# One layer slot reordered: both halves of P·V side by side, P's transposes into the third PSUM tile, the norm's Newton steps further down the vector queue

## The chip, the core and the metric

The kernel runs on one core of a Trainium2 chip. The time is what the device takes for one execution, in microseconds (us); the median of several executions is compared. The engines are named as the profile names them: PE is TensorE (PEld its weight loads), DVE is VectorE, ACT is ScalarE, POOL is GpSimd and SP is SyncE, which only issues DMAs here. Each engine runs its own queue in the order of the program and waits on semaphores where it needs another engine's result.

## The reference, cut to what matters

A causal attention block over 4 sequences of 512 tokens (width 128, 16 heads of 64) is followed by six layers. Each layer is local attention in windows of 32 tokens and a gated feed-forward network (FFN); both see their input with half of the features shifted by one token.

```python
def attn_layer(x, Wqkv, qs, ksc, Wo):          # x: 4 x 512 x 128
    q, k, v = split(x @ Wqkv)                  # 16 heads of 64
    q = l2norm(q) * qs
    k = l2norm(k) * ksc
    q = q * cos * scale + rotate_half(q) * sin * scale
    k = k * cos / scale + rotate_half(k) * sin / scale
    # every window of 32 tokens sees itself and the window before it
    sim = einsum('bhwie,bhwje->bhwij', q, look(k)) * 8
    out = einsum('bhwij,bhwje->bhwie', softmax(masked(sim)), look(v))
    return out @ Wo

def ffn_layer(x, g, bln, W1, b1, W2, b2):
    xn = (x - mean) / sqrt(var + 1e-05) * g + bln
    a, gate = split(xn @ W1 + b1)
    return a * gelu(gate) @ W2 + b2

for i in range(6):
    x = attn_layer(shift_tokens(x), ...) + x
    x = ffn_layer(shift_tokens(x), ...) + x
```

All of it is float32.

## The kernel before, in words

The first block (about the first 590 us) is not touched by the change. After it the work is cut into 96 **units**: layer, sequence b, and T, one of the four tiles of 128 tokens in a sequence. The function `slot` is called once for each unit, and the order of its calls is written out by hand: it is the order in which each engine's queue gets its instructions. Slot n works on several units at once, each at another stage:

- `new`, unit n+2: its three projections. `do_project(new, j)` with j = 0, 1, 2 for q, k, v is two products with 512 columns each (L477, of which the profile counts four). `square` (ACT, L488) and `sum_squares` (DVE, L493) give the squared norms. `rotate` is two DVE multiplications that read the projection in PSUM (L498 writes `rot`, L502 writes `t`). `add_rotated` (POOL, L513) adds them. `inverse_norms` takes 1/sqrt of the 32 sums: three short DVE instructions (L517, L80, L81), then twelve Newton steps on POOL (L83 to L86). `over_norm` (POOL, L521) scales. `v_windows` copies v out on ACT (L567), and SP issues 15 or 16 DMAs that spread it over the windows (`vw`).
- `nxt`, unit n+1: `transpose_q` and `transpose_k`, eight 128x128 transposes each (PE, L585) with two ACT copies (L588), and `carry_k` (POOL, L604), which hands the last 32 keys to the next unit.
- `u`, unit n: `scores` (the band mask L612 and the products L623, then DVE's maximum L633 and subtraction L635), `exponents` (ACT, L641), `transpose_p`, `times_v(u, 0)` and `times_v(u, 1)` (64 small products each, L655, then DVE's `rden` L664 and `on` L665), and `transpose_o`.
- `prev`, unit n-1: `project_out_2` (L680) and `residual` (L688).
- `now` and `last`, the FFN of the sequences before. With T = n % 4, `now` does `mean`, `var` and `scale` of its norm in the slots T = 1, 2, 3 (PE L94, L103, L111). `var` ends with `rsqrt`, that is L80, L81 and twelve Newton steps with four columns, all on DVE. `scale` is L115 and L117 on DVE. `chunk(0)` follows at T = 3; `last` does `chunk(1)`, `chunk(2)` and `out()` at T = 0, 1, 2 (L713 and L714, or L727), with DVE's L718 or L729 at the end.

`begin`, at the head of a slot, puts the shift of a coming sequence (L147 to L149) on POOL at T = 0, and once a layer also the rotary tables `lt` (L161).

PSUM decides what may overlap. Three tiles of two banks each rotate, `two_t(0)`, `two_t(1)`, `two_t(2)`; their roles move on by one from slot to slot. In a slot the first holds the scores, then v's projection, then the first half of P·V, then the FFN's chunk or `out()`. The second holds q's projection, then the second half of P·V. The third holds k's projection. Two single banks, `one_t()`, go round among the output projection, the norm, and all transposes. A tile is written again only when its readers are done: the second half of P·V waits for `rotate(new, 0)`, and the FFN's products wait for `on` of the first half.

Of the kernel before, what the change touches and what calls it, by code (L numbers as in the profile page):

```python
# [15 lines left out]
P = 128  # L16
# [4 lines left out]
NC = INNER // P  # L21
# [11 lines left out]
def body(ctx: ExitStack, tc: tile.TileContext, a, out: bass.AP):  # L33
# [5 lines left out]
    nc = tc.nc  # L39
# [3 lines left out]
    NT = S // P  # L43
# [31 lines left out]
    def rsqrt(v, n, eng):  # L75

        y = small.tile([P, n], F32, tag=f"y{n}", name="y")
        t = small.tile([P, n], F32, tag=f"yt{n}", name="yt")
        ti = t.bitcast(I32)
        nc.vector.tensor_scalar(ti, v.bitcast(I32), 1, None, ALU.logical_shift_right)  # L80
        nc.vector.tensor_scalar(y.bitcast(I32), ti, -1.0, 1597463007.0, ALU.mult, ALU.add)  # L81
        for k in range(3):
            eng.tensor_tensor(t, y, y, ALU.mult)  # L83
            eng.tensor_tensor(t, t, v, ALU.mult)
            eng.tensor_scalar(t, t, -0.5, 1.5, ALU.mult, ALU.add)
            eng.tensor_tensor(y if k < 2 else v, y, t, ALU.mult)  # L86

    def layernorm_steps(state, bank, inT, outT, g=None, b=None, eng=nc.vector):

        def mean():
            m = bank()
            mm(m, lhsT=avg, rhs=inT(), start=True, stop=True)  # L94
            xc = state["xc"] = tmpt()
            nc.vector.tensor_tensor(xc, inT(), m, ALU.subtract)
            sq = state["sq"] = tmpt()
            nc.scalar.activation(sq, xc, AF.Square)

        def var():  # L100
            v = bank()
            for t in range(NT):
                mm(v[:, t : t + 1], lhsT=state["sq"][:, t * P : (t + 1) * P], rhs=avg[:, 0:1], start=True, stop=True)  # L103
            rs = state["rs"] = small.tile([P, NT], F32, tag="rs", name="rs")
            nc.vector.tensor_scalar(rs, v[:, 0:NT], EPS, None, ALU.add)
            rsqrt(rs, NT, eng)

        def scale():
            bc = bank()
            for t in range(NT):  # L110
                nc.tensor.transpose(  # L111
                    bc[:, t * P : (t + 1) * P], state["rs"][:, t : t + 1].to_broadcast([P, P]), ident
                )
            h = state["h"] = outT()
            nc.vector.tensor_tensor(h, state["xc"], bc, ALU.mult)  # L115
            if g is not None:
                nc.vector.tensor_scalar(h, h, g, b, ALU.mult, ALU.add)  # L117

        return mean, var, scale

    xT = [None] * B

# [46 lines left out]
    with tc.manual_schedule():  # L169
# [70 lines left out]
        class Rows:  # L240
# [5 lines left out]
            def scores(self):  # L246
                b, c, t = self.b, self.c, self.t
                sc = self.sc = ps1.tile([P, 2, S], F32, tag="sc", name="ps_sc", bufs=2)
                for k0 in range(0, S, S // 2):
                    for h in range(2):  # L250
                        rows = slice(h * HD, (h + 1) * HD)
                        mm(
                            sc[:, h, k0 : k0 + S // 2],
                            lhsT=qs[b, c][rows, t * P : (t + 1) * P],
                            rhs=ks[b, c][rows, k0 : k0 + S // 2],
                            start=(k0 == 0),
                            stop=False,
                            skip_group_check=True,
                        )
# [23 lines left out]
            def exponents(self):  # L283
                self.pr = s1.tile([P, 2, S], F32, tag="pr1", name="pr1", bufs=3)
                self.den = small.tile([P, 2, 2], F32, tag="den", name="den")
                seen = (self.t + 1) * P
                for part_, cols in enumerate((slice(0, seen), slice(seen, S))):
                    for h in range(2):
                        if cols.start < S:
                            nc.scalar.activation(  # L290
                                self.pr[:, h, cols],
                                self.sc[:, h, cols],
                                AF.Exp,
                                bias=self.nm[:, part_, h : h + 1],
                                accum_out=self.den[:, part_, h : h + 1],
                            )
# [193 lines left out]
    def sum_squares(u, j):  # L490
        if j == 0:
            u.ss = small.tile([P, 2 * HEADS], F32, tag="ss", name="ss")
        nc.vector.tensor_reduce(u.ss[:, j * HEADS : (j + 1) * HEADS], heads(u.sq), AX.X, ALU.add)  # L493

    def rotate(u, j):
        t0 = u.r[j] = s2a.tile([P, INNER], F32, tag="rot", name="rot", bufs=6)
        lt, pf, half = u.lt, u.p[j], HD // 2
        nc.vector.tensor_tensor(  # L498
            heads(t0), heads(pf), lt[:, u.T, 2 * j].unsqueeze(1).to_broadcast([P, HEADS, HD]), ALU.mult
        )  # L500
        t1 = u.t1 = s2a.tile([P, INNER], F32, tag="t1", name="t1", bufs=3)
        nc.vector.tensor_tensor(  # L502
            t1.rearrange("p (h t d) -> p h t d", t=2, d=half),
            pf.rearrange("p (h t d) -> p h t d", t=2, d=half)[:, :, ::-1, :],
            lt[:, u.T, 2 * j + 1]
            .rearrange("p (t d) -> p t d", t=2)
            .unsqueeze(1)
            .to_broadcast([P, HEADS, 2, half]),
            ALU.mult,
        )  # L510
# [70 lines left out]
    def transposed(src, g, dst, col0):  # L581

        tp = one_t()
        for c in range(4):
            nc.tensor.transpose(  # L585
                tp[:, c * P : (c + 1) * P], src[:, (4 * g + c) * P : (4 * g + c + 1) * P], ident
            )
        nc.scalar.copy(dst[:, 4 * g : 4 * g + 4, col0 : col0 + P], tp.rearrange("p (c t) -> p c t", c=4))  # L588
# [53 lines left out]

    def transpose_p(u):
        u.pT = s2.tile([P, NC, P], F32, tag="pT", name="pT", bufs=2)
        for g in range(2):
            transposed(u.prf, g, u.pT, 0)

    def times_v(u, g):
        if g == 0:
# [43 lines left out]
    class Ffn:  # L693
        def __init__(self, i, b):
            self.i, self.b, self.us, self.st = i, b, [], {}
            self.mean, self.var, self.scale = layernorm_steps(
                self.st,
                one_t,
                lambda: self.xs,
                lambda: s2.tile([P, S], F32, tag="hT", name="hT", bufs=2),  # L700
                vecs[:, i, 0:1],
                vecs[:, i, 1:2],
            )

        def shift(self):
# [97 lines left out]
    def slot(n, now, last):  # L803

        u, prev, nxt, new = unit(n), unit(n - 1), unit(n + 1), unit(n + 2)
        T = n % NT
        part[0] = n % 3
        begin(unit(n + 4))  # L810
        if u:
            scores(u)
        if new:
            do_project(new, 0)
            square(new, 0)
        if n == -1:
            y = one_t()
            project_out1(B - 1, y)
        if u:
            exponents(u)  # L820
        if prev:
            project_out_2(prev)
            if prev.b + 1 == B and prev.T + 1 == NT and prev.i + 1 < L:
                wo_w[0] = load_wo(prev.i + 1)
        if new:
            sum_squares(new, 0)
        if prev:
            residual(prev)
        if now and T > 0:
            (now.mean, now.var, now.scale)[T - 1]()  # L830
        if now and T == 0:
            now.shift()
        if new:
            rotate(new, 0)
        if n == -1:
            residual1(B - 1, y)
        if new:
            do_project(new, 2)
            v_windows(new, follower(new))
        if u:  # L840
            transpose_p(u)
        if new:
            add_rotated(new, 0)
            do_project(new, 1)
            square(new, 1)
        if u:
            times_v(u, 0)
        if new:
            sum_squares(new, 1)
        if nxt:  # L850
            transpose_q(nxt)
        if u:
            times_v(u, 1)
        if new:
            inverse_norms(new)
            over_norm(new, 0)
        if nxt:
            transpose_k(nxt)
        if new:
            rotate(new, 1)  # L860
            add_rotated(new, 1)
            over_norm(new, 1)
        if n == -1:
            third_step()
        if nxt:
            carry_k(nxt, follower(nxt))
        if now and T == 3:
            now.chunk(0)
        if last:
            (lambda: last.chunk(1), lambda: last.chunk(2), last.out)[T]()  # L870
        if u:
            transpose_o(u)
# [106 lines left out]
```

## Time and profile before

| | |
|---|---|
| Time before, median of 3 runs | 2278.62 us (2278.29 to 2281.74) |
| Profiled execution | 2281.5 us, its span 2279.7 us |
| PE, DVE, ACT, POOL busy | 2178.0, 1729.1, 1347.6, 1451.3 us |
| Mean granted TensorE clock | 0.993 |
| From one band product to the next (a slot), median at T = 0, 1, 2, 3 | 16.6, 17.1, 18.7, 16.6 us |

The span runs from the first to the last instruction of the profiled execution. In a line of the timeline the first number is the start, the second the time that the instructions take, then come the engine, the source line, the operation, what is written from what, the count, and in brackets the idle time of the engine before it and who ended it. Line numbers are those of the kernel before.

### The profile page before, as it was taken

Reading aid. Unit: us, or ns where it says so; the run is one execution under the profiler, and the core shown is the slowest. Engines: PE = TensorE matmul, PEld = TensorE weight load, DVE = VectorE, ACT = ScalarE, POOL = GpSimd, SP = SyncE. Lnnn points to the kernel's source line nnn. Section 1 sums busy time; section 2 is a strip of 40 time slices with the busy share of each in tenths; the row PEclk is TensorE's granted clock in tenths of the full one; section 3 lists DMA queues with packets and bytes.
Section 4 is the critical chain, followed back from the end, with each engine's and each line's share of the span. In section 5 each row is a group of like instructions: output and inputs, shape, how many; then the busy total and the mean of one; then the engine's idle time right before and its main releaser. Section 6 shows DMA issues by size and latency. Waiting matters only on the chain.

```text
span 2279.7 us, 82205 instructions
## 1 busy us (share of the span) xinstructions
PE 2178.0 (96%) x35088; PEld 1435.6 (63%) x35088; DVE 1729.1 (76%) x2800; ACT 1347.6 (59%) x2550; POOL 1451.3 (64%) x1981
## 2 busy tenths in 40 slices
PE   6999999999999999999999999999999999999997
PEld 3555555555566666666666666666666666666664
DVE  3776667767778787878887788878888878888774
ACT  3665655655455656666566666666656666666562
POOL 1544545455877677767677777677776667766760
PEclk8999999999999999999999999999999999999998
DMA  3000000000322233232322323222332223222220
GB/s 115 1 1 1 1 1 1 1 1 1 75 70 64 63 88 75 58 75 68 87 67 64 77 70 91 64 62 69 85 85 56 72 63 88 73 67 70 65 56 15
DMA packets 91029, 125.74 MB, mean 55 GB/s; under 512 B 25390, under 2 KB 39468, under 8 KB 90668
## 3 DMA queue, kind: packets, MB, share of 16 engines
q1 hardware_dynamic: 90236, 118.92, 21.1%
q8 instruction: 279, 4.57, 0.9%
q10 hardware_dynamic: 432, 1.57, 0.2%
q14 instruction: 82, 0.67, 0.1%
HBM read 20.31 MB, written 1.05 MB: 9 GB/s over the span
## 4 chain that ended last, share of the span: by engine, by line
PE 63%; DVE 9%; issue 2%; ACT 1%; POOL 0%; POOLq 0%; ACTq 0%
PE ps_proj L477 19%; PE ps_one L585 14%; PE ps_one L680 7%; PE ps_att L655 6%; PE ps_att L623 6%; PE ps_proj L713 3%; PE ps_proj L714 3%; PE ps_proj L727 2%; DVE yt L80 2%; DVE t L502 1%; DVE rot L498 1%; PE ps_att L612 1%; PE ps_one L94 1%; PE ps_one L103 1%; DVE yt L83 1%
## 5 line engine op out<-in xcount | busy, mean ns | idle before, releaser
L513 POOL TENSOR_TENSOR rot<-rot,t 128x1024 f32<-128x1024 f32 x192 | 453.8, 2364 | 197.5 <-DVE t L502 185.9
L477 PE MATMUL ps_proj<-wqkv,xs 128*128 128x512 f32 x1152 | 553.3, 603 | 4.3 <-DVE t L502 2.8
L304 POOL TENSOR_TENSOR pr<-pr,den 128x1024 f32<-128x1024 f32 x128 | 240.9, 1893 | 266.9 <-DVE den L301 258.6
L488 ACT ACTIVATE sq<-ps_proj 128x1024 f32<-128x1024 f32 x192 | 196.8, 1025 | 356.7 <-PE ps_proj L477 324.5
L521 POOL TENSOR_TENSOR rot<-rot,ss 128x1024 f32<-128x1024 f32 x192 | 365.2, 1902 | 14.9
L477 PEld LDWEIGHTS ps_proj<-wqkv,xs 128*128 128x128 f32 x1152 | 198.1, 190 | 166.1 <-issue 146.5
L493 DVE TENSOR_REDUCE ss<-sq 128x16 f32<-128x1024 f32 x192 | 233.1, 1214 | 46.9 <-ACT sq L488 46.3
L498 DVE TENSOR_TENSOR rot<-ps_proj,lt 128x1024 f32<-128x1024 f32 x192 | 233.6, 1217 | 0.0
L502 DVE TENSOR_TENSOR t<-ps_proj,lt 128x1024 f32<-128x1024 f32 x192 | 233.2, 1215 | 0.4 <-POOL rot L513 0.4
L290 ACT ACTIVATE pr<-ps_sc,nm 128x128 f32<-128x128 f32 (+3 forms) x448 | 220.1, 507 | 20.0 <-DVE nm L279 16.7
L279 DVE TENSOR_REDUCE nm<-ps_sc 128x2 f32<-128x1024 f32 x128 | 156.0, 1219 | 91.0 <-PE ps_sc L267 91.0
L585 PE MATMUL ps_one<-ident,rot 128*128 128x128 f32 x1536 | 211.3, 280 | 5.9 <-issue 4.4
L680 PEld LDWEIGHTS ps_one<-aT,wo 128*128 128x128 f32 x1536 | 186.3, 192 | 45.3 <-issue 44.5
L83 POOL TENSOR_TENSOR yt<-y 128x32 f32<-128x32 f32 (+1 forms) x309 | 72.9, 236 | 210.5 <-DVE y L81 194.3
L633 DVE TENSOR_REDUCE mx<-ps_att 128x16 f32<-128x1024 f32 x96 | 117.5, 1224 | 102.3 <-PE ps_att L623 102.2
L680 PE MATMUL ps_one<-aT,wo 128*128 128x128 f32 x1536 | 187.3, 275 | 0.4 <-ACT aT L588 0.4
L585 PEld LDWEIGHTS ps_one<-ident,rot 128*128 128x128 f32 x1536 | 165.3, 141 | 25.3 <-issue 7.1
L319 ACT COPY pT<-ps_pt 128x512 f32<-128x512 f32 x128 | 75.5, 590 | 176.2 <-PE ps_pt L315 176.2
L655 PEld LDWEIGHTS ps_att<-vw,pT 64*32 64x32 f32 x9216 | 103.5, 105 | 93.4 <-ACT pT L588 54.0
L567 ACT COPY vt<-ps_proj 128x512 f32<-128x512 f32 x192 | 103.2, 590 | 93.6 <-PE ps_proj L477 91.6
L315 PEld LDWEIGHTS ps_pt<-ident,pr 128*128 128x128 f32 x1024 | 117.6, 142 | 56.7 <-issue 47.6
L655 PE MATMUL ps_att<-vw,pT 64*32 64x65 f32 x9216 | 129.0, 225 | 24.2 <-DVE t L502 13.4
(134 smaller groups left out, 4062.3 us busy)
## 6 DMA issues: line engine op xcount, KB each, us to landing
vw<-vt SPq DMA_DIRECT2D x1152, 65.0 KB
vw_first<-vt SPq DMA_DIRECT2D x336, 65.0 KB
wqkv<-in_wqkv_dram SPq DMA_DIRECT2D x18, 512.0 KB
wo<-in_wo_dram SPq DMA_DIRECT2D x6, 512.0 KB
w<-in_w_dram SPq DMA_DIRECT2D x6, 341.0 KB
xr<-in_x_dram SPq DMA_DIRECT2D x4, 256.0 KB
out_dram<-tmp_t SPq DMA_DIRECT2D x4, 256.0 KB
w<-in_w_dram SPq DMA_DIRECT2D x12, 64.0 KB
```

What stands on the lines that cost most here:

```text
L290: nc.scalar.activation(self.pr[:, h, cols], self.sc[:, h, cols], AF.Exp, bias=self.nm[:, part_, h : h + 1], accum_out=self.den[:, part_, h ...
L304: nc.gpsimd.tensor_tensor(self.pr, self.pr, self.den[:, 0].unsqueeze(2).to_broadcast([P, 2, S]), ALU.mult)
L477: mm(p[:, c, :], lhsT=u.xs[:, u.T * P : (u.T + 1) * P], rhs=wpart[j][:, c * 512 : (c + 1) * 512], start=True, stop=True,)
L488: nc.scalar.activation(u.sq, u.p[j], AF.Square)
L493: nc.vector.tensor_reduce(u.ss[:, j * HEADS : (j + 1) * HEADS], heads(u.sq), AX.X, ALU.add)
L498: nc.vector.tensor_tensor(heads(t0), heads(pf), lt[:, u.T, 2 * j].unsqueeze(1).to_broadcast([P, HEADS, HD]), ALU.mult)
L502: nc.vector.tensor_tensor(t1.rearrange("p (h t d) -> p h t d", t=2, d=half), pf.rearrange("p (h t d) -> p h t d", t=2, d=half)[:, :, ::-1, :],
L513: nc.gpsimd.tensor_tensor(u.r[j], u.r[j], u.t1, ALU.add)
L521: nc.gpsimd.tensor_tensor(heads(u.r[j]), heads(u.r[j]), u.ss[:, j * HEADS : (j + 1) * HEADS].unsqueeze(2).to_broadcast([P, HEADS, HD]), AL ...
L585: nc.tensor.transpose(tp[:, c * P : (c + 1) * P], src[:, (4 * g + c) * P : (4 * g + c + 1) * P], ident)
L655: mm(o[j * W : (j + 1) * W, h, c * (HD + 1) : (c + 1) * (HD + 1)], lhsT=u.pT[h * HD : (h + 1) * HD, 4 * g + c, j * W : (j + 1) * W], rhs=u ...
L680: mm(y[:, 0:P], lhsT=wo_w[0][:, c, :], rhs=u.aT[:, c, :], start=(c == 0), stop=(c == NC - 1))
```

## The change

Three things are reordered in `slot`, and nothing is computed differently.

1. `times_v(u, 0)` and `times_v(u, 1)` stand together, after `transpose_q` and before k's projection; before, q's transposes stood between them. k's projection, `square(new, 1)`, `rotate(new, 1)`, `add_rotated(new, 1)`, `sum_squares(new, 1)`, `inverse_norms` and both `over_norm` come after them, the POOL work after `carry_k`.
2. `transpose_p` writes its eight transposes into `two_t(2)` instead of the two single banks, and both ACT copies follow the last transpose.
3. The norm's `rsqrt` is a fourth step, `roots`, called at T = 2 after `rotate(new, 0)`, `add_rotated(new, 0)` and `sum_squares(new, 0)`.

`exponents(u)` also moves ahead of q's projection, and `sum_squares(new, 0)` behind `rotate(new, 0)`.

```diff
@@ layernorm_steps
             rs = state["rs"] = small.tile([P, NT], F32, tag="rs", name="rs")
             nc.vector.tensor_scalar(rs, v[:, 0:NT], EPS, None, ALU.add)
-            rsqrt(rs, NT, eng)
+            if not apart:
+                roots()
+
+        def roots():
+            rsqrt(state["rs"], NT, eng)
...
@@ transpose_p
         u.pT = s2.tile([P, NC, P], F32, tag="pT", name="pT", bufs=2)
+        tp = two_t(2, "ps_att")
+        for c in range(NC):
+            nc.tensor.transpose(
+                tp[:, c // 4, c % 4 * P : (c % 4 + 1) * P], u.prf[:, c * P : (c + 1) * P], ident
+            )
         for g in range(2):
-            transposed(u.prf, g, u.pT, 0)
+            nc.scalar.copy(u.pT[:, 4 * g : 4 * g + 4], tp[:, g].rearrange("p (c t) -> p c t", c=4))
...
@@ slot
         if u:
             scores(u)
+            exponents(u)
         if new:
             do_project(new, 0)
             square(new, 0)
...
-        if u:
-            exponents(u)
         if prev:
             project_out_2(prev)
...
-        if new:
-            sum_squares(new, 0)
-        if prev:
             residual(prev)
...
         if new:
             rotate(new, 0)
+            add_rotated(new, 0)
+            sum_squares(new, 0)
...
+        if now and T == 2:
+            now.roots()
         if new:
             do_project(new, 2)
             v_windows(new, follower(new))
         if u:
             transpose_p(u)
-        if new:
-            add_rotated(new, 0)
-            do_project(new, 1)
-            square(new, 1)
-        if u:
-            times_v(u, 0)
-        if new:
-            sum_squares(new, 1)
         if nxt:
             transpose_q(nxt)
         if u:
+            times_v(u, 0)
             times_v(u, 1)
         if new:
-            inverse_norms(new)
-            over_norm(new, 0)
+            do_project(new, 1)
+            square(new, 1)
         if nxt:
             transpose_k(nxt)
-        if new:
-            rotate(new, 1)
-            add_rotated(new, 1)
-            over_norm(new, 1)
         if n == -1:
             third_step()
         if nxt:
             carry_k(nxt, follower(nxt))
+        if new:
+            rotate(new, 1)
+            add_rotated(new, 1)
+            sum_squares(new, 1)
+            inverse_norms(new)
+            over_norm(new, 0)
+            over_norm(new, 1)
```

More of the change, by code (lines that the diff above doesn't have):

```diff
@@ L86, in rsqrt, with layernorm_steps @@
             eng.tensor_tensor(y if k < 2 else v, y, t, ALU.mult)
-    def layernorm_steps(state, bank, inT, outT, g=None, b=None, eng=nc.vector):
+    def layernorm_steps(state, bank, inT, outT, g=None, b=None, eng=nc.vector, apart=False):
         def mean():
@@ L117, in scale @@
                 nc.vector.tensor_scalar(h, h, g, b, ALU.mult, ALU.add)
-        return mean, var, scale
+        return (mean, var, scale, roots) if apart else (mean, var, scale)
     xT = [None] * B
@@ L695, in __init__ @@
             self.i, self.b, self.us, self.st = i, b, [], {}
-            self.mean, self.var, self.scale = layernorm_steps(
+            self.mean, self.var, self.scale, self.roots = layernorm_steps(
                 self.st,
@@ L702, in __init__ @@
                 vecs[:, i, 1:2],
+                apart=True,
             )
```

## The prediction

> **What bounds the kernel now.** I read four views, in this order. First the page: busy time and the chain that ended last.
>
> ```profile
> PE 2178.0 (96%) x35088; PEld 1435.6 (63%) x35088; DVE 1729.1 (76%) x2800; ACT 1347.6 (59%) x2550; POOL 1451.3 (64%) x1981
> ...
> PE 63%; DVE 9%; issue 2%; ACT 1%; POOL 0%; POOLq 0%; ACTq 0%
> ```
>
> TensorE (PE) carries the chain, so in the layers a slot (one unit of 128 tokens) lasts as long as its PE work plus PE's waits. I then read the timeline between successive band products (L612), which open every slot: median 16.6 us at T=0, 17.1 at T=1, 18.7 at T=2 and 16.6 at T=3. T=2 has two more products (L727), 0.86 us; about 0.8 us more is a wait. The timeline of one T=2 slot (start 1445.17) shows it:
>
> ```profile
> 1451.60 1.90 POOL L521 TENSOR_TENSOR rot<-rot,ss 128x1024 f32<-128x1024 f32 x1
> 1451.63 0.16 DVE L105 TENSOR_SCALAR rs<-ps_one 128x4 f32<-128x4 f32 x1
> 1451.83 1.70 DVE L80 TENSOR_SCALAR yt<-rs 128x4 int32<-128x4 int32 x1
> ...
> 1456.17 1.22 DVE L498 TENSOR_TENSOR rot<-ps_proj,lt 128x1024 f32<-128x1024 f32 x1
> 1456.73 1.09 PE L585 MATMUL ps_one<-ident,rot 128*128 128x128 f32 x8
> 1457.30 1.21 DVE L502 TENSOR_TENSOR t<-ps_proj,lt 128x1024 f32<-128x1024 f32 x1
> ...
> 1458.57 0.86 PE L655 MATMUL ps_att<-vw,pT 64*32 64x65 f32 x64 [0.74 <-DVE t L502]
> ```
>
> The norm's root stands on VectorE (DVE) ahead of `rotate(new, 0)`: L80 to the last L86 take 4.3 us (1451.83 to 1456.17). `rotate` therefore ends at 1458.51, and only then may the second half of P·V write the bank that q's projection held. Note L80: 1.70 us for four columns, where the 128x32 form has a median of 0.18. It ended when GpSimd's (POOL's) L521 ended (1453.50).
>
> The same thing is seen once a layer with other instructions, where POOL is late:
>
> ```profile
> 1633.87 2.35 POOL L513 TENSOR_TENSOR rot<-rot,t 128x1024 f32<-128x1024 f32 x1
> 1633.97 2.29 DVE L517 TENSOR_SCALAR ss<-ss 128x32 f32<-128x32 f32 x1
> 1636.29 0.18 DVE L80 TENSOR_SCALAR yt<-ss 128x32 int32<-128x32 int32 x1
> 1636.51 0.18 DVE L81 TENSOR_SCALAR y<-yt 128x32 int32<-128x32 int32 x1
> 1636.60 1.22 DVE L498 TENSOR_TENSOR rot<-ps_proj,lt 128x1024 f32<-128x1024 f32 x1
> ```
>
> A small tensor_scalar of DVE stands still until the POOL instruction that runs beside it is over. The rotations, which read PSUM, keep 1.21 to 1.22 us whatever POOL does.
>
> [...]eight transposes take 0.87 us from start to start beside whole-array work, 1.02 to 1.03 between the two halves of P·V, 0.93 after one.
>
> **The change, part by part.** Times within a slot count from its band products. Pitches from the PE timeline: scores 1.85, projection 1.82 after a tiled block and 1.72 otherwise, output projection 1.78, norm 0.86/0.81/0.44 (T=1/2/3), eight transposes 0.87, half of P·V 0.79, an FFN chunk 1.72, L727 2.58.
>
> *P·V in one block.* Before: P 0.87, projection of k 1.81, half 0.79, q 1.03, half 0.79, K 0.93, sum 6.22. After: P 0.87, q 0.96, halves 1.58, projection 1.82, K 0.87, sum 6.10. That is -0.12 in each of some 93 slots. P's transposes go to the third tile, whose chunk of the slot before is long read; ScalarE (ACT) copies them out by about 10.2, before k's projection needs the tile (11.5). q's transposes cover those copies except for some 0.1.
>
> *Exponentials ahead of q's projection in program order* (its square follows on ACT): at T=0 the table load (1.28) no longer stands between square and exponentials, and a PE wait of 0.2 before P's transposes goes (the V projection there has a pitch of 1.92). SP's 15 or 16 copies to `vw` follow the same ACT copies at the same point of the slot and are read two slots later: nothing.
>
> *`sum_squares(new, 0)` behind `rotate(new, 0)`*: 1.14 of DVE off rotate's path; outside T=2 nothing waited there.
>
> *The POOL chain.* Each instruction of the k side now comes after k's projection, which is itself later. At T=1: projection ends 13.3; rotate on DVE 13.5 to 15.85; ACT squares (1.02) before it copies K out, so `carry_k`, now ahead of `add_rotated(new, 1)` on POOL, runs 15.7 to 16.15; the add 16.2 to 18.55 (2.36). `inverse_norms` is now issued 0.7 us behind the start of that add: L517 is ready at 17.0 and stands still until 18.55, in every slot and not once a layer. L81 starts at 19.0, POOL's twelve Newton steps at 19.3 (12 x 0.32), over_norm at 23.1 and 25.0, end 26.85, which is 10.1 us into the T=2 slot. In the kernel before, over_norm(1) ended at 8.3 of that slot.
>
> *Roots later, T=2.* DVE: rotate(0) 6.65 to 8.95, its sum of squares to 10.05, then the roots. POOL's add_rotated(0) starts at 10.1 and ends at 12.45. L80 or, if that slips through, L81 stands still until then; twelve steps of 0.2 give 15.0. Queued behind the roots is rden/on of the first half (0.24 + 0.69): 15.9. The order of instructions confirms that `last.out`'s first product waits for DVE: it writes the tile that this half holds. PE is ready at 1.85+1.82+1.78+0.81+1.72+0.87+0.96+1.58+1.82+0.87 = 14.1. New wait: 1.8 us, in place of 0.8. T=2: -0.12 + 1.0 = +0.9.
>
> *T=3 after it.* rotate(1) now runs 16.8 to 19.1, the blocked L517 ends at 21.6, the residual L729 holds DVE to 22.8, while the scores are done at 19.5 + 1.85 = 21.4. The maximum starts 1.4 late; the subtraction ends about when V's projection wants the tile (+0.1). The norm's L117, also a tensor_scalar in SBUF, comes 4.0 to 4.1 us after L81, and over_norm(0) starts 0.26 + 3.86 = 4.1 us after it: a toss-up. If L117 is second it waits 1.9, rotate(0) ends at 11.1 and the second half of P·V, due at 10.3, waits 0.8; if first, nothing.
>
> *T=0*: the 0.2 gained goes again on V's projection waiting for the late subtraction and q's transposes for over_norm (0.1 each).
>
> *Once a layer* POOL's `lt` (2.37) stands before add_rotated(0) and now pushes the whole chain to q's transposes: +0.8, five times.
>
> Sum per four slots: T=0 -0.1, T=1 0, T=2 +0.9, T=3 +0.1 or +0.9; together +0.9 or +1.7. Over 23 sequences +21 or +39, with the layers' +4: +25 or +43. The toss-up taken in the middle: **+33 us**. The profiled execution has 2279.7 us of span and 1.8 around it, 2281.5; that gives 2314.5. It ran 2.9 above the median of 2278.6, so I predict **2311 us**.
>
> [...]
>
> **Rivals.**
> *The roots meet an idle POOL (faster).* [...]the roots end at 12.5 and `on` at 13.4, before PE wants it at 14.1. T=2 then gains 0.9, T=3 none or 0.1: with T=0 and T=1 about -1.2 per four slots, -28 us, 2251 us. For it: L80 on `ss` has a median of 0.18 where POOL is idle. Against: in all T=2 slots L80 took 0.94 to 1.84, and POOL has work queued at that point. It decides if `on` ends before 14.1, so if add_rotated(0) ends before 10.6 instead of 12.45.
>
> *The two waits are equal (no change).* If over_norm ends 1 us earlier than laid out, add_rotated(0) ends at 11.4 and the new wait is 0.8; savings and the rest of T=3 cancel: within 5 us, 2276.
>
> *POOL's chain sets every slot (much slower).* From k's projection to q's transposes the chain takes 0.2+2.35+2.4+0.75+3.9+1.9, and PE's 0.96+1.58+1.82 back to the end of that projection: 15.9, plus carry_k's delay 0.3, so 16.2 against PE's own 15.95 at T=0 and 16.8 at T=1. With 0.3 more on POOL, all slots but T=2 lengthen: +0.65 per slot, 2340 us. For it: equality at T=0. Against: T=1 and T=2 have slack.
>
> **How the numbers follow.** A measurement of this kernel can tell about 0.2%, 4.6 us, from no change. Port wait at the roots and at L517, 0.75: 2311, own range 2293 to 2332. Much slower 0.06. Equal waits 0.06, of which 0.04 within the bound, the rest either side of it. Idle POOL 0.13. The range, 2268 to 2338, takes in the equal waits and part of the way to 2251. Faster 0.14, same 0.04, slower 0.82.
>
> **What would show it.** At T=2: L80 or L81 on `rs` at 2 us and more behind L513; the wait of L655 for DVE `t` gone, and a wait of `last.out`'s products for DVE `on` of 1.5 to 2 us. L517 with a mean near 1.7 us instead of 0.21. No transposes of 1.03 us between halves of P·V. At T=3 L117 either near 2 us, with the second half waiting for `t`, or near 0.3. If L80 on `rs` stays under 1 us and `last.out` doesn't wait, the forecast is wrong and the faster rival holds.

## The result, and the profile after

The changed kernel takes 2427.21 us (median of 6 runs, 2420.58 to 2435.3) against 2280.53 us for the kernel before on the same chips (6 runs, 2278.29 to 2281.91). The ratio is 1.0646, with a 95% interval of 1.0624 to 1.0669: slower by 147 us. The forecast was 2311, with a range of 2268 to 2338. The direction was right; the loss is over four times as large as forecast (33), and outside the range.

In the changed file the source lines named here lie 5 to 11 further down: scores L628 (before L623), subtraction L640 (L635), P·V L665 (L655), `rden`/`on` L674/L675, square L493, `sum_squares` L498, `rotate` L503/L507, `add_rotated` L518, `inverse_norms` L522, `over_norm` L526, scale of the norm L122 (L117), projection L482, transposes of P L652 with their copies L656, other transposes L590 with copies L593, `out()` L738. L80 and L81 keep theirs.

The first view is the page of the changed kernel: busy time, and the chain that ended last.

```profile
PE 2249.6 (93%) x35088; PEld 1511.9 (62%) x35088; DVE 1834.2 (76%) x2800; ACT 1319.2 (54%) x2550; POOL 1456.8 (60%) x1981
...
PE 43%; DVE 22%; issue 6%; ACT 4%; POOL 2%; SPq 0%; DMA 0%; ACTq 0%; POOLq 0%
```

With the same instructions, PE counts 72 us more and DVE 105 us more, PE's share of the chain falls from 63% to 43%, DVE's rises from 9% to 22%, and "issue", where an engine waits for nothing that the profile shows, from 2% to 6%. (PE's ends are modelled, and the count of products is the same: a longer busy time here means the same products drawn out, not more work.) The loss stands in the layers: from the first band product to the last it is 145 us. Of this, 6.5 us lie in the first slot and 8.7 in two slots near the end; in the other slots a mean of 17.3 us has become 18.7. Where the slots lose, in mean us from start to start over 20 or 21 slots each (the first eight and the last six of the 96 left out):

| | T=0 | T=1 | T=2 | T=3 |
|---|---|---|---|---|
| slot, before | 16.60 | 17.24 | 18.57 | 17.03 |
| slot, after | 17.71 | 19.16 | 20.41 | 17.80 |
| both halves of P·V, before | 1.79 | 1.70 | 1.61 | 2.04 |
| both halves of P·V, after | 2.27 | 3.03 | 2.86 | 2.99 |

P·V has 4.0 of the 5.6 us per four slots. The waits of PE over the layers (PE and what it writes, line, releaser: us in all, times, longest; "issue" as the releaser means that the profile shows none) show one half of this. Of the kernel before:

```profile
PE ps_att L655 <- DVE t L502: 13.4, 18, 1.5
PE ps_att L655 <- issue: 10.1, 12, 1.6
...
PE ps_att L623 <- issue: 6.2, 14, 1.7
```

and of the kernel after:

```profile
PE ps_att L665 <- issue: 47.0, 27, 2.6
PE ps_att L628 <- issue: 20.5, 28, 2.0
PE ps_proj L738 <- DVE rden L674: 15.2, 14, 2.0
PE ps_proj L482 <- DVE pr L640: 14.1, 19, 1.4
```

The wait for `t` has gone, and the wait of `out()` (L738) for DVE has come, as laid out in the prediction. But the largest idle time of PE stands inside P·V and inside the scores, and no semaphore ends it. The timeline of T=1 and the start of T=2 (slots at 1433.16 and 1452.95) shows the rest:

```profile
1444.67 1.09 ACT L656 COPY pT<-ps_att 128x512 f32<-128x512 f32 x2
1445.33 2.31 PE L665 MATMUL ps_att<-vw,pT 64*32 64x65 f32 x128
...
1449.65 1.03 ACT L493 ACTIVATE sq<-ps_proj 128x1024 f32<-128x1024 f32 x1 [2.91 <-PE ps_proj L482]
1450.71 1.23 DVE L503 TENSOR_TENSOR rot<-ps_proj,lt 128x1024 f32<-128x1024 f32 x1 [1.91 <-ACT sq L493]
1453.15 2.36 POOL L518 TENSOR_TENSOR rot<-rot,t 128x1024 f32<-128x1024 f32 x1 [1.05 <-DVE t L507]
1454.22 1.32 DVE L522 TENSOR_SCALAR ss<-ss 128x32 f32<-128x32 f32 x1
```

This P·V has no gap, and yet it lasts 2.31 us, 2.24 from its start to the next block's; two halves alone took 2 x 0.79 from start to start. And DVE's rotation L503 starts 0.03 us after ACT's square L493 has ended: it stands still for a reader of the same PSUM tile. L522 then starts 1.07 us into POOL's L518 and ends 0.03 us after it. This is what the prediction calls the port wait; that a port is what holds these instructions is not shown. From 600 us on, 23 of the 25 L80 with four columns take over 0.5 us in the kernel before and end 0.02 to 0.03 us after a POOL instruction that ran beside them, and in the kernel after all 94 L522 end 0.04 us after L518. Divided into stretches of 0.4 us (busy PE and PEld with their instructions, clock, DMA share, GB/s), one P·V of the changed kernel goes like this:

```profile
1445.30:1445.70 0.40, 0.37 (x7) 0.37 (x8) 1.00 0.82 328
1445.70:1446.10 0.40, 0.40 (x10) 0.40 (x8) 1.00 0.93 369
1446.10:1446.50 0.40, 0.40 (x39) 0.40 (x37) 1.00 0.72 264
1446.50:1446.90 0.40, 0.40 (x61) 0.40 (x41) 1.00 0.80 249
```

Its first 17 products take 0.8 us, the pace after that is several times as high. The clock granted is full (1.00) all the while. The head of the block is slow.

### The profile page after: what moved, and what is told of

Same layout as the page of the kernel before. It is cut to its first block, busy times and chain, and to the rows that moved or that the text cites. A ratio compares the mean times of both kernels' runs of the same rounds, so it can differ in the third digit from the quotient of the medians.

```text
span 2425.6 us, 82264 instructions
## 1 busy us (share of the span) xinstructions
PE 2249.6 (93%) x35088; PEld 1511.9 (62%) x35088; DVE 1834.2 (76%) x2800; ACT 1319.2 (54%) x2550; POOL 1456.8 (60%) x1981
## 4 chain that ended last, share of the span: by engine, by line
PE 43%; DVE 22%; issue 6%; ACT 4%; POOL 2%; SPq 0%; DMA 0%; ACTq 0%; POOLq 0%
PE ps_proj L482 15%; PE ps_att L665 7%; PE ps_one L590 5%; PE ps_one L690 3%; DVE rot L503 3%; DVE t L507 3%; DVE ss L498 3%; PE ps_att L628 3%; ACT sq L493 3%; DVE ss L522 3%; PE ps_proj L738 2%; DVE pr L640 2%; PE ps_att L652 2%; DVE mx L638 2%; DVE yt L80 1%
## 5 line engine op out<-in xcount | busy, mean ns | idle before, releaser
L518 POOL TENSOR_TENSOR rot<-rot,t 128x1024 f32<-128x1024 f32 x192 | 453.5, 2362 | 260.2 <-DVE t L507 244.9
L482 PE MATMUL ps_proj<-wqkv,xs 128*128 128x512 f32 x1152 | 579.4, 626 | 21.5 <-DVE pr L640 17.4
L503 DVE TENSOR_TENSOR rot<-ps_proj,lt 128x1024 f32<-128x1024 f32 x192 | 234.6, 1222 | 236.9 <-ACT sq L493 236.6
L493 ACT ACTIVATE sq<-ps_proj 128x1024 f32<-128x1024 f32 x192 | 194.9, 1015 | 346.3 <-PE ps_proj L482 345.6
L526 POOL TENSOR_TENSOR rot<-rot,ss 128x1024 f32<-128x1024 f32 x192 | 365.2, 1923 | 7.4
L482 PEld LDWEIGHTS ps_proj<-wqkv,xs 128*128 128x128 f32 x1152 | 199.5, 192 | 204.1 <-issue 160.9
L646 ACT ACTIVATE pr<-pr 128x1024 f32<-128x1024 f32 x96 | 101.5, 1057 | 356.1 <-DVE pr L640 356.1
L507 DVE TENSOR_TENSOR t<-ps_proj,lt 128x1024 f32<-128x1024 f32 x192 | 233.2, 1214 | 6.9 <-POOL rot L518 6.9
L498 DVE TENSOR_REDUCE ss<-sq 128x16 f32<-128x1024 f32 x192 | 232.0, 1208 | 0.0
L590 PEld LDWEIGHTS ps_one<-ident,rot 128*128 128x128 f32 x1536 | 179.0, 144 | 65.3 <-issue 54.4
L665 PE MATMUL ps_att<-vw,pT 64*32 64x65 f32 x9216 | 172.2, 226 | 45.3 <-issue 42.9
L590 PE MATMUL ps_one<-ident,rot 128*128 128x128 f32 x1536 | 207.1, 279 | 2.9 <-POOL rot L526 1.7
L665 PEld LDWEIGHTS ps_att<-vw,pT 64*32 64x32 f32 x9216 | 150.7, 106 | 65.2 <-issue 46.2
L675 DVE TENSOR_TENSOR on<-ps_att,rden 128x512 f32<-128x512 f32 x192 | 132.8, 692 | 6.6
L320 PE MATMUL ps_pt<-ident,pr 128*128 128x128 f32 x1024 | 134.6, 274 | 3.0 <-POOL pr L309 2.9
```

The lines of the kernel that those rows point to most:

```text
L320: nc.tensor.transpose(pt[:, k * P : (k + 1) * P], self.pr[:, h, k * P : (k + 1) * P], ident)
L482: mm(p[:, c, :], lhsT=u.xs[:, u.T * P : (u.T + 1) * P], rhs=wpart[j][:, c * 512 : (c + 1) * 512], start=True, stop=True,)
L493: nc.scalar.activation(u.sq, u.p[j], AF.Square)
L503: nc.vector.tensor_tensor(heads(t0), heads(pf), lt[:, u.T, 2 * j].unsqueeze(1).to_broadcast([P, HEADS, HD]), ALU.mult)
L507: nc.vector.tensor_tensor(t1.rearrange("p (h t d) -> p h t d", t=2, d=half), pf.rearrange("p (h t d) -> p h t d", t=2, d=half)[:, :, ::-1, :],
L518: nc.gpsimd.tensor_tensor(u.r[j], u.r[j], u.t1, ALU.add)
```

## The experiments

Three theories for the slow block. **D**: its first eight products, two for each of the four windows, wait on the semaphores of the DMAs that filled `vw`. These have long landed (those issued in the slot before 1357.67 had moved their data by 1362, and the P·V that reads them starts at 1386.46), but most waits are an instruction of their own on PE's queue. The line view of the kernel after has them (durations in ns, shortest, median and longest; first and last start):

```profile
L665 PEldq EVENT_SEMAPHORE  x691: 51/51/51, 726.2 to 2267.3; - x173
```

**S**: 128 small products in a row (and their 128 weight loads) outrun the supply of instructions. **T** (the theory, not the tile number): the DMA traffic of that stretch slows the products. The expectations name a fourth, **V**: the chain of DVE and POOL has become longer. If it were that alone, none of the edits to P·V would help.

**a_split: the two halves apart again.** In the kernel after, k's projection between them.

```diff
             times_v(u, 0)
-            times_v(u, 1)
         if new:
             do_project(new, 1)
+        if u:
+            times_v(u, 1)
+        if new:
             square(new, 1)
```

> The changed kernel with one edit: k's projection stands between the two halves of P.V, so no more than 64 small products follow one another. Measured for the changed kernel: 2427 us; 25 gaps in the 128-product block in which PE waits for nothing that the profile shows, 44 us together, and a block pitch of 2.2 us where it has no such gap. Theory S (a run of 128 products, 256 PE instructions with their weight loads, outruns the supply of instructions): the gaps fall to about what the kernel before had in its halves (7 us), and the time by 35 to 50 us, to 2375 to 2390. Theory D (the first eight products each wait for DMAs, and nothing covers that any longer): the first half still takes 1.3 to 1.4 us instead of 0.8, second half 0.8. Theory V (the vector and GpSimd chain is what became longer): within 10 us of 2427.

Measured: 2370.89 us, ratio to the kernel before 1.0396 [1.038, 1.0411], 56 us less than the kernel after and so more than V allows.

```profile
PE ps_att L665 <- issue: 4.8, 8, 2.0
```

The gaps in P·V fall from 47.0 to 4.8 us, as S has it. The first half still takes 1.31 (T=0) to 1.58 us (T=1), the second 0.79 by median: the slow head stays with the first half, as D has it. Two different things had been put together.

**b_join: the halves joined in the kernel before.** k's projection and q's transposes then stand ahead of the block, and nothing else is changed.

```diff
             square(new, 1)
-        if u:
-            times_v(u, 0)
         if new:
             sum_squares(new, 1)
...
         if u:
+            times_v(u, 0)
             times_v(u, 1)
```

> The kernel before with one edit: both halves of P.V stand together, after q's transposes; k's projection and q's transposes still lie between P's transposes and the block. Theory S: gaps of about 2 us in the block as in the changed kernel, some 25 of them, time 2310 to 2330. Theory D: the waits are dealt with while PE still works on the projection, the block pitch is 1.6, time 2265 to 2280 ([...]the wait at T=2 in the same place). Theory V: the same as D.

Measured: 2298.49 us, ratio 1.0074 [1.0055, 1.0093], between the ranges of S and D. By median the block takes 1.53 to 1.69 us at T=0, T=1 and T=3 (at T=2 it waits for `t` and takes 2.72): the head is not slow here, with the same DMA waits. The difference is in what stands ahead. In one slot of b_join, ACT's copies of P are done 1.56 us before the block:

```profile
1431.37 1.10 ACT L588 COPY pT<-ps_one 128x512 f32<-128x512 f32 x2
...
1434.03 1.64 PE L655 MATMUL ps_att<-vw_first,pT 64*32 64x65 f32 x128
```

In the kernel after, the block starts before the second of these copies is done (1445.33 against 1445.76, above). PE's queue stands at the wait for P until PE has run dry (0.32 us of idle time of PEld before the block, ended by the first copy), and the DMA waits come only then. In b_join the queue goes through them while PE still works on k's projection and q's transposes (1431.35 to 1434.03). The line views of these two blocks show it, first the kernel after, then b_join:

```profile
L665 PEldq EVENT_SEMAPHORE  x7: 51/51/51, 1445.3 to 1446.1; - x7
```

```profile
L655 PEldq EVENT_SEMAPHORE  x6: 51/51/51, 1432.5 to 1433.5; - x6
```

Seven waits lie in the first 0.8 us of the one block (it starts at 1445.33), 0.125 us apart; six lie 0.5 to 1.5 us ahead of the other (1434.03). Gaps of 20.2 us (16 of them; before 10.1, 12 of them) stay in b_join, and so joining alone is a loss of 18 us.

**a_spare and a_nodma: P·V without DMA waits.** In the kernel after, P·V reads a tile filled once with ones instead of `vw`, so v is left out of the result. a_spare still issues the window copies (into two buffers instead of three); a_nodma issues none.

```diff
-                        rhs=u.vw[h * HD : (h + 1) * HD, j, 4 * g + c, :],
+                        rhs=vw_still[0][h * HD : (h + 1) * HD, j, 4 * g + c, :],
```

> The changed kernel, with P.V reading a fixed window buffer that is filled once with ones; all window copies of v are still issued, to buffers that nothing reads. So the traffic is the same and P.V waits for no DMA; the values of v are left out of the result. Theory D: the block without a gap falls from 2.2 to about 1.6 us, 55 us in all, to about 2370. Theory S: the gaps stay at about 44 us together. Theory T (the traffic of the window copies delays PE's instruction supply): they stay as well. Theory V: within 10 us of 2427.

> As the kernel with the fixed window buffer, but the window copies are not issued at all, so that their traffic is gone too; v's values are left out of the result. Theory T: the 2 us gaps in the block vanish (under 8 us together) and the time falls by a further 45 to 60 us against the run with the traffic, to about 2315. Theory S (length of the run alone): the gaps stay and the time is within 10 us of the run with the traffic.

Measured, one run each: 2358.87 and 2353.11 us, against 2280.85 for the kernel before on that chip. The wait instructions at P·V fall from 796 to 93. In a_spare the block takes 1.53 to 1.59 us, except at T=3, where it waits for `t` and takes 2.4, and the gaps in it shrink from 47.0 to 0.9 us. Without the traffic too it takes 1.45. D holds: of the 2.0 to 2.3 us of a block without a gap, some 0.6 are the DMA waits and 0.1 is the traffic, so T is worth some 6 us, from one run each. But only 68 us come back. The faster block meets the next wait, `out()` for DVE at T=2:

```profile
PE ps_proj L742 <- DVE rden L678: 31.3, 15, 2.3
PE ps_proj L482 <- DVE pr L644: 20.5, 27, 1.4
```

(`out()` is L742 here, the V projection's releaser L644 is the subtraction.) Those are waits on DVE that the slow P·V had hidden (15.2 and 14.1 us in the kernel after).

**a_touch: the same waits, met elsewhere.** In the kernel after, four products of one column read the windows of `vw` right after the output projection and write unused columns of its tile. All is still computed.

```diff
             project_out_2(prev)
+            for j in range(NW if u else 0):
+                mm(prev.y[0:HD, P + j : P + j + 1], lhsT=u.vw[:, j, 0, 0:HD], rhs=u.vw[:, j, 0, 0:1], start=True, stop=True)
```

> The changed kernel plus four products of one column per slot, right after the output projection, which read the four windows of v that P.V will need and write unused columns of the output projection's bank. Nothing of the result changes; PE meets the waits for the window DMAs there, 4 us before P.V, and P.V itself waits for copies of ScalarE and VectorE alone. Theory D (the bare DMA waits at the head of the block cost 0.6 us a slot, and they use up PE's lead, so that hiccups in instruction supply show): as in the run without those waits, block at about 1.6 us, gaps in it under 5 us, 2355 to 2370. Theory S (length of the run alone): gaps stay at some 44 us, over 2400. Theory V: within 10 us of 2427.

Measured: 2363.03 us, ratio 1.0361 [1.0345, 1.0376]. One block, in the timeline of a_touch:

```profile
1556.89 1.59 PE L665 MATMUL ps_att<-vw,pT 64*32 64x65 f32 x128
```

No gap is left in any of them. The four added products take 0.56 to 0.67 us in the mean and the output projection ahead of them 0.1 more, which is about what the block has saved: the price is paid again in the new place (how much of it is the waits and how much the products is not separated). So the 64 us are in the main the gaps: 47.0 us in P·V are gone, and of the 20.5 in the scores 17.8 are left.

**a_touch_rot: the rotation of k ahead of its square.** On top of a_touch.

```diff
             do_project(new, 1)
-            square(new, 1)
...
             add_rotated(new, 1)
+            square(new, 1)
             sum_squares(new, 1)
```

> The kernel with the early waits, plus one more edit: square(new, 1) is called after rotate(new, 1) and add_rotated(new, 1), so that the rotation no longer waits until ScalarE has squared the same PSUM tile (0.26 us latency and 1.02 us of square). Theory Q (that wait lengthens the chain rotation, add, port wait, Newton steps, over_norm by 1 us in every slot, which is the part of the loss that my sum had left out): the wait of V's projection for the subtraction at T=0 (0.6 us) and half of the wait of last.out at T=2 go, -0.6 us per slot or -45 to -60 us against the kernel with the early waits, to 2300 to 2315. Rival (the loss is at the roots and the port only): within 10 us of the kernel with the early waits.

Measured: 2327.9 us, ratio 1.0208 [1.019, 1.0227], 35 us less than a_touch: a gain was expected, but a larger one. In the kernel after, DVE waited for squares of ACT like this over the layers (a_touch, on which this edit stands, has 172.8 us, 132 times; about two thirds stand ahead of k's rotation, the rest of q's):

```profile
DVE rot L503 <- ACT sq L493: 229.8, 140, 3.7
```

and in a_touch_rot:

```profile
DVE rot L503 <- ACT sq L493: 21.2, 30, 1.1
```

What is left stands ahead of q's rotation. Part of the wait has moved and not gone: `sum_squares` now waits 117.3 us for the square, and the rotation 41.1 for k's projection, but the rotation and POOL behind it no longer stand behind the square. The wait of V's projection for the subtraction, 5.0 us in a_touch, is gone, and K's transposes at T=2 fall from 2.49 to 1.79 us. L522 is short again: in the groups of instructions by form (busy, mean ns) it had

```profile
L522 DVE TENSOR_SCALAR ss<-ss 128x32 f32<-128x32 f32 x83 | 109.8, 1323 | 2.9
```

in the kernel after (a mean of 1321 ns in a_touch), and has in a_touch_rot

```profile
L522 DVE TENSOR_SCALAR ss<-ss 128x32 f32<-128x32 f32 x78 | 15.0, 192 | 2.7
```

So the wait for the square and the wait of L522 went in one edit; what each is worth alone is not separated.

**sp_rotfirst: the same edit without the DMA waits.** On top of a_spare, so v is left out here too.

> The changed kernel with P.V reading the fixed window buffer (v's values are left out of the result, traffic unchanged) and square(new, 1) behind rotate(new, 1). Against the kernel with the early waits and the same reordering (2328 us) only the four early products are missing, which took 0.55 to 0.66 us of PE per slot. Theory D (the DMA waits cost PE about 0.6 us a slot wherever no earlier work covers them, in the block or in the early products): 2270 to 2300, with longer waits for DVE at T=2 and T=3 taking part of it back. Rival (the early products only use time in which PE would wait anyway): within 10 us of 2328.

Measured, one run: 2295.09 us beside 2283.01 for the kernel before: 64 us below a_spare. With both causes gone, 12 us of the loss are left. The slots are 16.11, 17.18, 19.34 and 17.07 us: T=2 is the one that is clearly longer than before (by 0.77), and there K's transposes with the wait of `out()` take 2.42.

**a_touch_rot_pool and b_pool: the FFN norm's Newton steps on POOL.** One argument (`eng=nc.gpsimd`) in `layernorm_steps`, on top of a_touch_rot and in the kernel before.

> As the last, and the norm's twelve Newton steps run on GpSimd instead of VectorE, at the same place in program order. Theory R (the roots that stand before rden and on at T=2 hold the tile that last.out writes): its wait falls from about 1.4 us to 0, -1.5 to -2.3 us at each T=2, -35 to -50 us, to 2255 to 2275, below the kernel before. Rival (GpSimd's queue is full: add_rotated(1) comes later by the steps' 3.9 us and the wait goes to q's transposes at T=3): no gain.

> The kernel before with one edit: the Newton steps of the FFN's norm run on GpSimd, L80 and L81 stay on VectorE at the same place. Theory R (what delayed rotate(0) at T=2 are the steps): the wait of the second half of P.V for t (0.65 us on average, up to 0.99) goes in 22 slots, -12 to -20 us, 2260 to 2268. Rival (the delay is the port wait of L80, which stays, or GpSimd's add_rotated comes later and delays a transpose): within 5 us of 2280.

Measured: 2321.87 us, ratio 1.0175 [1.016, 1.019], only 6 us below a_touch_rot, where more was expected; and 2267.72 us, ratio 0.9942 [0.9927, 0.9957], as expected. In the first, the wait of `out()` goes (T=2 from 19.39 to 18.47), but at T=3 the norm's L122 now takes longer. Its group in a_touch_rot and in a_touch_rot_pool:

```profile
L122 DVE TENSOR_SCALAR hT<-hT,vecs 128x512 f32<-128x512 f32 x20 | 21.0, 1048 | 0.7
```

```profile
L122 DVE TENSOR_SCALAR hT<-hT,vecs 128x512 f32<-128x512 f32 x20 | 34.4, 1718 | 0.7
```

That it waits beside a POOL instruction there is likely, not shown: in the kernel after, from 600 us on, 21 of 24 L122 take over 0.8 us (median of all 1.70, shortest 0.55), and each of the 21 ends 0.28 us after POOL's `over_norm` (L526). P·V at T=3 then takes 2.25 instead of 1.65 us, waiting for `t` and for ACT's copy of q: of the 0.9 us that T=2 gives, T=3 takes 0.7. In the kernel before L122's counterpart gets shorter instead (L117 has a mean of 0.75 us in b_pool, 1.26 before), and b_pool is 13 us faster than the kernel before: T=2 falls from 18.57 to 17.98.

**b_roots: the later roots alone.** In the kernel before, `roots` after `rotate(new, 0)` at T=2, as in the change (the order of `sum_squares` and `add_rotated` kept).

> The kernel before with one edit: the norm's root is called after rotate(new, 0) and not in var; everything else keeps its place. Theory R1 (alone, this part is a gain: the wait of the second half of P.V at T=2, 0.65 us on average, goes; the roots[...] end some 2.5 us before last.out needs the tile, since k's projection and q's transposes still lie between): 2262 to 2275. Rival R2 (also alone it is a loss: the roots delay rden, on and the start of the k side's Newton steps, and the next slot's projection or transposes wait): 2285 to 2300.

Measured: 2285.57 us, ratio 1.001 [1.0002, 1.0018]. That is just inside R2's numbers, but only 2.6 us above the kernel before as measured beside it (2283.01), so neither a gain nor a loss of the size expected. In q's transposes with the wait behind them, 1.66 us become 1.02, but K's transposes, behind which `out()` waits, go from 0.93 to 1.21, the second half from 0.81 to 0.99, and T=3 lengthens by 0.2. This part of the change is worth about nothing by itself; its waits only change places.

**b_pool_exp: exponentials first at T=0, on top of b_pool.**

```diff
             scores(u)
+            if T == 0:
+                exponents(u)
```

> The kernel before with the norm's Newton steps on GpSimd (2268 us alone) and, at T=0 only, exponents(u) ahead of q's projection in program order, so that the activation table is loaded while PE still makes the scores. Theory: V's projection and P's transposes at T=0 take 1.72 and 0.87 instead of 1.92 and 0.93, -6 us, 2260 to 2264. Rival (the square, and with it the sum of squares and rotate(0), come later and the second half of P.V waits for t): no gain or a loss.

Measured: 2287.86 us, ratio 1.0019 [1.0011, 1.0027], 20 us above b_pool (18 against the kernels before measured beside each): a miss. V's projection falls to the expected 1.72, but P's transposes at T=0 take 2.31:

```profile
PE ps_one L585 <- ACT pT L588: 26.8, 22, 1.2
```

The square comes later on ACT, `sum_squares` waits for it on DVE, and `residual` behind it ends some 0.8 us after the first four transposes have begun, where in b_pool it ended 1 us ahead of them. The second four wait for `residual` in b_pool; here they wait for ACT's copy of the first four, and start 0.05 us after it. That the late `residual` is the reason for this other wait is likely but not shown. In the changed kernel `residual` stands ahead of `sum_squares` and P's transposes have another tile; there they take 0.91 us at T=0.

**b_join_touch: the added products in b_join.**

> The kernel before with both halves of P.V together (2298 us; 12 gaps, 17 us, in the block) plus the four early products, so that the block of 128 products has no DMA wait at its head. Theory S2 (the gaps come from the length of the run alone): 12 gaps or so stay. Theory D2 (a gap needs the waits at the head of the run as well): fewer than 4 gaps stay; the early products add 0.5 to 0.6 us per slot, so the time is 2315 to 2340 all the same.

Measured, one run: 2331.39 us, a time as expected. The gaps in P·V fall from 20.2 us (16) to 4.7 (9), while the products read the same data at the same length of run. Nine gaps are fewer than S2 wants and more than D2 does: the DMA waits at the head matter, and they aren't all.

**What PE waits for in the gaps.** The traces kept of these runs show it. The page of the kernel after has a DMA queue of the kind "instruction" (transfers, MB, share of 16 engines):

```profile
q8 instruction: 280, 4.59, 0.8%
```

Each transfer has 16384 bytes. The trace has 71,674 instructions of PE and PEld, the semaphore instructions among them, so one transfer brings 256 of them (280 x 256 = 71,680): as many as a block of P·V has products and weight loads. From 600 us on, the kernel after has 58 idle times of PE of 0.2 us and more that no semaphore ends. All 58 end at one and the same place in every 256 of that count (to within one), and 1.2 to 1.5 us after the landing of a transfer. One of them, in the T=2 slot that starts at 1452.95:

```profile
1462.89 1.74 PE L665 MATMUL ps_att<-vw,pT 64*32 64x65 f32 x124
1466.65 0.30 PE L665 MATMUL ps_att<-vw,pT 64*32 64x65 f32 x4 [2.02 <-issue]
```

The transfer ran from 1464.14 to 1465.26. So PE stands still for its next instructions, and S names the right thing. Which blocks are hit goes with when the transfer starts: in the kernel after it starts over 1.4 us ahead of the block 70 times, without a gap, and 0.2 us ahead of it or later 27 times, and these are the 27 gaps. In a_spare it is late twice in 95 blocks, and these two have a gap; in a_touch it never is, and there is none. (The line between early and late is not as clean in b_join: there 16 of the 18 latest are hit.) In 23 of the 27 it starts 1.1 to 2.4 us into the block, behind the DMA waits of its head. Whether the waits hold back the transfer as well as the products, and what makes a transfer start, is not shown.

## Why the prediction was wrong in size

*Joined P·V, "halves 1.58" and "q's transposes cover those copies except for some 0.1".* This step failed, and it is the larger part. Its term of -0.12 per slot was the sum of pitches seen in another order. Three measurements stand against it: the block takes 2.0 to 2.3 us where it isn't interrupted (mean 2.17), so some 0.6 us more in each of some 95 slots, about 56 us; the gaps in P·V grow by 47.0 - 10.1, 37 us; and those in the scores by 20.5 - 6.2, 14 us, though these belong as much to the next step (17.8 us in a_touch, 6.1 in a_touch_rot). The prediction put SP's copies at "nothing" because they are read two slots later. The data was indeed there; but their semaphores are waited for by instructions on PE's queue, and k's projection, which had covered these, was moved behind the block. b_join and a_spare show both sides. The prediction had no term for the supply of PE's instructions, to which the gaps belong (all 58 at one place in every 256). The other pitches came out about as laid out: by median q's transposes 0.97 to 1.02 (1.17 at T=1), K's 0.87 but for T=2, k's projection 1.82.

*The POOL chain, "projection ends 13.3; rotate on DVE 13.5 to 15.85".* This step failed too, by one instruction: the square of k lies between, and rotation starts when it ends. In the trace of the kernel after L503 waits 140 times for the square, 229.8 us in all, and each time starts 0.03 us after it has ended, though both only read the tile. Some 150 us (76 times) of this are k's rotation, and of each wait the square itself (1.02 us) is only a part. That makes everything behind it about 1 us later, and puts the subtraction at T=0 late: V's projection begins 0.57 us later after the start of the output projection than before (1.78 to 2.35), where 0.1 was forecast. The way back was worth 35 us in a_touch_rot, 64 in sp_rotfirst. The parts add up to 142 to 171 us (56 + 37 + 14, and 35 to 64) beside the 147 measured. As a late P·V hides waits on DVE, they overlap, and are no ledger to the microsecond. T=1, which the prediction put at 0 in its sum without giving a reason, lost most (1.92 us a slot).

*L522 beside POOL's add* (L517 before, the forecast's port wait) was right: a mean of 1.32 us in place of 0.21, where about 1.7 was forecast.

*Roots later at T=2* was right in kind: the wait of P·V for `t` is gone and `out()` waits for DVE. K's transposes, with that wait behind them, go from 0.93 to 1.78 us, a wait of 0.85 in the mean against the forecast's 1.8, since P·V itself is late; where it isn't (a_spare), 2.2. L80 on four columns took less than the 2 us named for it:

```profile
L80 DVE TENSOR_SCALAR yt<-rs 128x4 int32<-128x4 int32 x20 | 31.2, 1562 | 0.0
```

*T=3* was called a toss-up. L122 has a mean of 1.64 us (x21), the late side; its price of 0.8 us on P·V is seen in a_spare, but in the kernel after the block's own slowness covers most of it.

*What was not forecast at all* is that the loss of one part hides the loss of another. None of the rivals was this: the nearest in time, the POOL chain that sets every slot (2340), was given 0.06 and put the whole cause on POOL; PE's waits for POOL before its transposes are 1.7 us in all. With the DMA waits and the square out of the way (sp_rotfirst, one run), the kernel stands 12 us above the one before; there T=2 is 0.77 us longer, where the forecast had 0.9. (The middle of +25 and +43 is 34, not 33; that is of no weight.)

## What to carry to other kernels

A transfer that landed long ago still cost where its semaphore was waited for (the block took 2.0 to 2.3 us with these waits at its head, 1.53 to 1.59 without them in a_spare): when work is moved to the place right behind another wait, count the wait instructions at its head, and ask what the engine has left to do while its queue goes through them. Where an engine is idle and no semaphore ends it, look at when its instructions were transferred: here the 256 instructions of one block of small products, as many as one transfer brought, were used up in 2.0 to 2.3 us. When a step is moved behind another on one tile of PSUM, list every reader of that tile: here the second reader, L503, started 0.03 us after the first had ended. And a sum of durations from one order of the program holds for another only if what stands ahead of each block is the same.

## What the runs showed of the hardware that was not expected

- A semaphore instruction on PE's queue took 51 ns (all 691 at P·V in the layers of the kernel after). At the head of P·V they came 0.125 us apart, with two products between them, and the block of 128 products took 2.0 to 2.3 us where PE had nothing left to do; it took 1.53 to 1.69 where the queue went through them while PE still worked (b_join), and 1.53 to 1.59 without them (a_spare but for T=3).
- PE's instructions came in transfers of 16384 bytes, 256 instructions each (280 transfers and 71,674 instructions in the kernel after, 279 and 71,587 in the kernel before). From 600 us on, PE took up a new 256 no earlier than 1.16 us after their landing in the kernel after and 1.22 us in the kernel before, and a transfer took 0.9 to 1.8 us. In the kernel after, where it started 0.2 us ahead of the block or later (27 times), P·V stood still for up to 2.6 us, and the profile names no releaser.
